# A mixture-of-experts kernel on one core: the order of the routed experts written by hand, and a shared expert in the tail that computes all gates first

## The chip, the cores and the metric

The kernel runs on one core of a Trainium2 chip. The metric is device time in microseconds (us) of one execution. Each number quoted as "the time" is a median of several executions; the profile is one further execution, with the hardware profiler on.

## The reference

Input `x` is four batches of 512 tokens with 512 features, all in float32. There are two residual stages.

```
x = x + tanh(g_xattn) * quantised_mlp(layernorm(x), fside, ctx)      # int8 "smooth quant" GLU, 512 -> 2*256 -> 512
x = x + tanh(g_ffn)   * moe(layernorm(x), gate_w, w_gate, w_up, w_down, ws_gate, ws_up, ws_down)
```

The second stage is a mixture of experts over all 2048 tokens:

```
scores = softmax(x @ gate_w.T)                 # 16 experts; each token takes its best 2
buf[e] = up to 256 tokens that chose expert e  # 16 x 256 x 512
y_e    = (silu(buf[e] @ w_gate[e]) * (buf[e] @ w_up[e])) @ w_down[e]   # 512 -> 352 -> 512
y      = sum over the token's two experts of weight * y_e
sh     = (silu(x @ ws_gate) * (x @ ws_up)) @ ws_down                   # shared expert, 512 -> 704 -> 512
return y + sh
```

## The kernel before, in words

The program is one straight line of instructions, some 6,000 in all, with no loop on the chip. It has five parts.

**Opening (0 to 75 us).** Batch 0 goes through the quantised stage. The order is written out with times (`Program`, lines 43 to 56).

**Plan (75 to 312 us).** Batches 1 to 3 go through the quantised stage, tokens are scored and routed, and the shared expert of batches 0 to 2 fills TensorE between. Each step has an engine, an assumed duration, the steps it needs and a rank. `Plan.run` (lines 83 to 116) keeps a clock for each engine, always takes the step that can begin first, and of those ready on one engine the one with the lowest rank; then it emits the steps in that order. `takes` says that a step needs a free buffer of a kind, `gives` which step frees it; `margin` is how late a TensorE step is assumed to see a result of another engine. Scores and routing have ranks from `ROUTE` = 1e5, the shared expert from `SHARED` = 1e6 (line 1049).

**Routed experts (312 to 551 us).** Loop over 16 experts, lines 1402 to 1419. An expert's gate and up products are done by a Winograd-like scheme: the 512x352 weights are cut in halves, four sums of weight halves (`combine_weights`, four VectorE subtractions, lines 1293 to 1296) and four sums of token halves (`combine_tokens`, lines 1333 to 1336) are formed, and seven products of two matmuls each (`product`, line 1342) replace eight. I number these P1 to P7 in the order of `gate_up`: P1 = b1 from `A11,Bg`, P2 = b2 from `A12,Dg`, P3 adds `S2,T2` onto b1, P4 = b3 from `S1,T1`, P5 adds `S3,T3` onto b1, P6 adds `A22,T4` onto b1, P7 adds `S4,Du` onto b3. Since P3, P5 and P6 accumulate onto b1, ScalarE must have copied b1 out before each of them: `p1` (line 1362) before P3, `u2` (line 1369) before P5, `u3` (line 1372) before P6. Between the copies `p1` and `u2`, ScalarE has the activation `g1` (line 1367), which needs VectorE's sum `p1 + b2` (line 1366).

Between P5 and P6, TensorE transposes the next expert's 256 gathered tokens (`turn_tokens`, `tp_g`, line 1322). After P7 come the down projection of the expert before (`down_routed`, `eo`, line 902) and the transposes of this expert's features (`turn_features`, `tp_h`, line 1391, copied out on VectorE at line 1392 into `ehT`). GpSimd gathers the tokens of expert e+2 by an indirect DMA (`gather`, line 1306). Weights `wg`, `wu`, `wd` of expert e+2 are loaded on the SP queue into one of two buffers each (lines 975 to 980).

Outside a `tc.manual_schedule()` block the framework's own scheduler decides the order of the instructions on each engine, and may put them far from where they stand in the program; inside such a block the order is that of the program. The opening, the plan and the tail are in such blocks; the loop over the experts is not. `combine_weights(e + 1)` stands after P2 of expert e in the program (line 1365), and `routing_weights` (lines 865 to 876: one Exp on ScalarE and nine small VectorE operations, the two combine weights of each token) after expert 1 (line 1419).

**Tail (551 to 625 us).** The shared expert of batch 3, and the gathers of the experts' results. It is 4 chunks of 128 features after chunk 0: for each chunk four gate matmuls (`pg`), Silu, four up matmuls (`pu`), then their product on VectorE into `hT` (line 894); then a rest of 64 features (`pr`, line 926, product at line 933); then four token tiles of six matmuls each (`sh`, line 947), the fifth-numbered chunk being the rest. GpSimd gathers 32 result tiles `yk` (line 1438) into 25 buffers; VectorE adds each to `X` (line 1449), in the order of the token tiles 0 to 15, and each finished tile is stored. How many adds stand ahead of each next step on VectorE is written by hand in line 1459: 6, 13, 19, 21, 26, 28, 30, 32, 32.

Of the kernel before, what the change touches and what calls it, by code (L numbers as in the profile page):

```python
# [20 lines left out]
P = 128  # L21
B, S, H = 4, 512, 512
HC = H // P
# [96 lines left out]
def flamingo_gated_kernel(  # L120
# [758 lines left out]
    def glu_steps(xT, o, dst):  # L879


        v = SimpleNamespace(ps={})
# [6 lines left out]
        def silu():  # L889
            v.g = shp.tile([P, S], F32, tag="g", name="g", bufs=2)  # L890
            act.activation(v.g, v.ps["pg"], AF.Silu)  # L891
# [14 lines left out]
    def shared(b, done=None):  # L906
        s = SimpleNamespace()

        def chunk_steps(c):
            if c == 0:  # L910
                s.hT = shp.tile([P, len(CHUNKS_IS), S], F32, tag="hT", name="hT")
            return glu_steps(xTs[b], c * P, s.hT[:, c, :])
# [30 lines left out]
        def tokens_product(t, c):  # L943
            if c == 0:
# [3 lines left out]
                accs[t], lhsT=s.hT[:m, c, bass.ts(t, P)], rhs=wsd[:m, c, :], start=(c == 0), stop=(c == FULL)  # L948
# [20 lines left out]

    E_W = {}  # L970

    def load_expert(e):
# [4 lines left out]
        nc.sync.dma_start(out=wu, in_=w_up[e].rearrange("(k p) i -> p k i", p=P))  # L977
        wd = ep.tile([P, len(CHUNKS_I), H], F32, tag="wd", name="wd")
        nc.sync.dma_start(out=wd[:, :2, :], in_=w_down[e, : 2 * P, :].rearrange("(c p) h -> p c h", p=P))
        nc.sync.dma_start(out=wd[: I - 2 * P, 2, :], in_=w_down[e, 2 * P :, :])  # L980
        E_W[e] = wg, wu, wd
# [283 lines left out]
    def experts_weights():  # L1265
# [3 lines left out]
        load_expert(0)  # L1269
        load_expert(1)  # L1270

    ep = None
    plan.add("SP", 3.0, experts_weights, firsts[B - 1].last, rank=0.0)
    with tc.manual_schedule():
        planned = plan.run()

    R = [SimpleNamespace() for _ in range(E)]
    HALF = HC // 2

    pair = []

    def combine_weights(e):


        r = R[e]
        wg, wu, _ = E_W[e]  # L1290
        pl, tag = (ep, "T") if e % 2 == 0 else (shp, "hT")
        T = pl.tile([P, 3, HALF, I], F32, tag=tag, name="T", bufs=1)
        vec.tensor_tensor(T[:, 0], wu[:, :HALF, :], wg[:, :HALF, :], ALU.subtract)  # L1293
        vec.tensor_tensor(T[:, 1], wu[:, HALF:, :], T[:, 0], ALU.subtract)
        vec.tensor_tensor(wu[:, :HALF, :], wu[:, HALF:, :], wu[:, :HALF, :], ALU.subtract)
        vec.tensor_tensor(T[:, 2], wg[:, HALF:, :], T[:, 1], ALU.subtract)
        r.T1, r.T2, r.T4, r.T3 = T[:, 0], T[:, 1], T[:, 2], wu[:, :HALF, :]
        r.Bg, r.Dg, r.Du = wg[:, :HALF, :], wg[:, HALF:, :], wu[:, HALF:, :]

    def gather(e):  # L1300
        r = R[e]
        r.xg = []
# [203 lines left out]
```

## Time and profile before

| what | value |
|---|---|
| time before, median of 3 | 621.93 us (621.26 to 623.81) |
| the profiled execution's own time | 627.15 us |
| its span, first to last instruction | 625.4 us |
| TensorE (PE) busy in the span | 572.3 us, 92% |
| VectorE (DVE) busy | 417.1 us, 67% |
| ScalarE (ACT) busy | 169.5 us, 27% |
| GpSimd (POOL) busy | 140.7 us, 22% |
| mean TensorE clock granted | 0.971 of full |
| bytes moved | 83.4 MB, mean 133 GB/s |

How to read it. A float32 matmul appears in the trace as two MATMUL instructions, so four matmuls of a gate chunk are "x8". A line of the timeline gives the start, the time covered, engine, source line, operation, tiles, shapes and count, and in brackets the idle time just before it with what ended that idle time. In the chain of waits a line is start, length and what the end of the program hung on then. In a table of windows the columns are the stretch, its length, TensorE's busy time with its instruction count, the granted clock (1.00 is full), the busy share of the DMA engines, and GB/s. "PEld" is a weight load, which lies beside matmuls. A matmul's end is modelled, so the distance from start to start is the safer measure of what TensorE takes.

### The profile page before, as it was taken

To read this page: it belongs to the slowest core of one execution; us is meant where nothing else is said; L and a number is where in the kernel's file an instruction comes from. 1 tells how busy PE (TensorE), PEld (TensorE's weight loads), DVE (VectorE), ACT (ScalarE), POOL (GpSimd) and SP (SyncE) were. 2 spreads that over 40 slices of the span, in tenths; PEclk is the share of its full clock that TensorE was granted. 3 is DMA by queue.
4 is the path that set the end of the run, shared out by engine and by line. 5 is a ranking of instruction groups with operands and counts; after the bars stand their busy time and mean duration, and the time that the engine had idled before them with its cause. 6 is when DMAs were issued, how large, how long until landed. Compare 5 with 4: busy or idle time off the path is not lost.

```text
span 625.4 us, 6259 instructions
## 1 busy us (share of the span) xinstructions
PE 572.3 (92%) x2068; PEld 309.8 (50%) x2068; DVE 417.1 (67%) x913; ACT 169.5 (27%) x323; POOL 140.7 (22%) x183
## 2 busy tenths in 40 slices
PE   1444999999989999999999999999999999999987
PEld 0322554445545644644365556556556666544422
DVE  6998979999998587473187555556656666313563
ACT  3543354336343520420021222222222222211000
POOL 1223122450432223002021111111111100005770
PEclk9976899999999999899999999999999999999989
DMA  8941110110000450102056666766666664215882
GB/s 304 343 169 40 62 38 31 35 68 1 1 1 0 162 184 1 68 1 67 0 168 214 199 206 214 230 206 212 206 206 205 206 205 127 80 44 163 280 282 105
DMA packets 47103, 83.40 MB, mean 133 GB/s; under 512 B 4880, under 2 KB 23312, under 8 KB 47072
## 3 DMA queue, kind: packets, MB, share of 16 engines
q1 hardware_dynamic: 37344, 57.84, 28.3%
q0 software_dynamic: 5120, 16.78, 9.3%
q10 hardware_dynamic: 4608, 8.39, 3.6%
q8 instruction: 16, 0.26, 0.2%
q14 instruction: 15, 0.12, 0.1%
HBM read 66.23 MB, written 16.78 MB: 133 GB/s over the span
## 4 chain that ended last, share of the span: by engine, by line
PE 66%; DVE 19%; DMA 6%; POOL 4%; issue 3%; ACT 2%; SPq 0%; DVEq 0%; ACTq 0%
PE b L1342 18%; PE sh L947 12%; PE eo L902 9%; PE pg L887 8%; PE pu L887 6%; DMA wu<-in_L_ffn_w_up_dram 4%; POOL yk L1438 3%; PE logit L721 2%; PE tp_g L1322 2%; PE tp_q L353 2%; DVE amw L383 1%; PE tp_x L707 1%; PE acc L533 1%; DMA wi<-in_fside_BxS2xS_dram 1%; DVE bn L284 1%
## 5 line engine op out<-in xcount | busy, mean ns | idle before, releaser
L947 PE MATMUL sh<-wsd,hT 128*128 128x512 f32 x192 | 93.4, 619 | 3.0 <-DVE hT L933 3.0
L902 PE MATMUL eo<-wd,ehT 128*128 128x512 f32 (+1 forms) x192 | 85.3, 592 | 0.0
L887 PE MATMUL pg<-xT,wsg 128*128 128x512 f32 x160 | 78.0, 619 | 0.0
L887 PE MATMUL pu<-xT,wsu 128*128 128x512 f32 x160 | 74.7, 596 | 0.0
L1306 POOL DMA_INDIRECT xg<-xn_dram,slot_token x32 | 31.9, 997 | 145.4 <-PE tp_g L1322 107.9
L902 PEld LDWEIGHTS eo<-wd,ehT 128*128 128x128 f32 (+1 forms) x192 | 36.5, 190 | 41.8 <-issue 38.4
L947 PEld LDWEIGHTS sh<-wsd,hT 128*128 128x128 f32 x192 | 33.7, 192 | 47.2 <-issue 42.2
L1342 PE MATMUL b<-wu,S 128*128 128x352 f32 x128 | 43.9, 466 | 2.3 <-ACT u L1369 2.3
L887 PEld LDWEIGHTS pg<-xT,wsg 128*128 128x128 f32 x160 | 30.0, 197 | 29.8 <-issue 28.8
L887 PEld LDWEIGHTS pu<-xT,wsu 128*128 128x128 f32 x160 | 29.5, 191 | 30.4 <-issue 29.7
L1438 POOL DMA_INDIRECT yk<-eo_dram,slot x32 | 33.6, 1051 | 39.1 <-PE pg L887 29.7
L1399 ACT COPY eo_sb<-eo 128x512 f32<-128x512 f32 x32 | 18.7, 585 | 86.1 <-PE eo L902 62.2
L1342 PE MATMUL b<-wg,xgT 128*128 128x352 f32 x128 | 40.8, 460 | 0.4 <-DVE xgT L1323 0.4
L1342 PE MATMUL b<-T,S 128*128 128x352 f32 x128 | 40.5, 459 | 0.0
L1375 DVE TENSOR_TENSOR u<-u,b 128x352 f32<-128x352 f32 x16 | 8.3, 521 | 43.2 <-ACT u L1372 43.2
L1293 DVE TENSOR_TENSOR T<-wu,wg 128x704 f32<-128x704 f32 x16 | 14.3, 891 | 33.1 <-DMA wu<-in_L_ffn_w_up_dram 33.1
L1449 DVE SCALAR_TENSOR_TENSOR X<-yk,wk,X 128x512 f32<-128x512 f32 x32 | 23.6, 751 | 15.9 <-DMA yk<-eo_dram,slot 15.7
L1342 PEld LDWEIGHTS b<-wu,S 128*128 128x128 f32 x128 | 23.5, 190 | 18.5 <-ACT u L1369 7.3
L891 ACT ACTIVATE g<-pg 128x512 f32<-128x512 f32 x20 | 11.9, 594 | 71.7 <-PE pg L887 71.7
L1342 PEld LDWEIGHTS b<-T,S 128*128 128x128 f32 x128 | 24.4, 190 | 13.5
L953 DVE SCALAR_TENSOR_TENSOR X<-sh,tg_f,X 128x512 f32<-128x512 f32 x16 | 12.0, 747 | 25.3 <-PE sh L947 25.1
L1359 POOL MEMSET h_e<- 128x32 f32 x32 | 4.0, 124 | 110.1 <-PE tp_h L1391 98.8
(207 smaller groups left out, 913.8 us busy)
## 6 DMA issues: line engine op xcount, KB each, us to landing
wg<-in_L_ffn_w_gate_dram SPq DMA_DIRECT2D x16, 704.0 KB, 4.6
wu<-in_L_ffn_w_up_dram SPq DMA_DIRECT2D x16, 704.0 KB, 4.5
wd<-in_L_ffn_w_down_dram SPq DMA_DIRECT2D x16, 512.0 KB, 4.6
eo_dram<-eo_sb ACTq DMA_DIRECT2D x32, 256.0 KB, 3.0
X<-in_x_dram SPq DMA_DIRECT2D x16, 256.0 KB, 8.5
wi<-in_fside_BxS2xS_dram SPq DMA_DIRECT2D x4, 1024.0 KB, 7.3
xn_dram<-y SPq DMA_DIRECT2D x16, 256.0 KB, 2.1
out_dram<-X SPq DMA_DIRECT2D x16, 256.0 KB, 3.9
```

The costliest lines, as they stand in the source:

```text
L353: pe.transpose(tps[k // 2][:, k % 2, t, :], qbits[:, t, bass.ts(k, P)], ident_h)
L721: pe.matmul(pl_t[:, :E], lhsT=xTs[b][:, k, bass.ts(t, P)], rhs=gateT[:, k, :], start=(k == 0), stop=(k == HC - 1),)
L887: pe.matmul(v.ps[name], lhsT=w[:, k, o : o + P], rhs=xT[:, k, :], start=(k == 0), stop=(k == HC - 1))
L902: pe.matmul(acc, lhsT=hT[:m, c, bass.ts(t, P)], rhs=wd[:m, c, :], start=(c == 0), stop=(c == len(chunks) - 1))
L947: pe.matmul(accs[t], lhsT=s.hT[:m, c, bass.ts(t, P)], rhs=wsd[:m, c, :], start=(c == 0), stop=(c == FULL))
L1293: vec.tensor_tensor(T[:, 0], wu[:, :HALF, :], wg[:, :HALF, :], ALU.subtract)
L1306: pool.indirect_dma_start(out=xg, out_offset=None, in_=xn_dram, in_offset=bass.IndirectOffsetOnAxis(ap=slot_token[:, c : c + 1], axis=0),)
L1322: pe.transpose(tp[:, k, :], r.xg[h][:, bass.ts(k, P)], ident)
L1342: pe.matmul(ps[:, :I], lhsT=lhs[:, k, :], rhs=rhs[:, k, :], start=(first and k == 0), stop=(k == HALF - 1), skip_group_check=not first,)
L1399: act.copy(eo, acc)
L1438: pool.indirect_dma_start(out=yk, out_offset=None, in_=eo_dram, in_offset=bass.IndirectOffsetOnAxis(ap=slot[i % 2][:, i // 2 : i // 2 + 1] ...
L1449: vec.scalar_tensor_tensor(X[:, j, :], yks[i], wk[k][:, j : j + 1], X[:, j, :], ALU.mult, ALU.add)
```

## The change

The mathematics is the same. What changes is order and buffers.

1. `load_expert` is split into `load_gate_up` and `load_down`. `load_gate_up(e + 2)` is issued at the end of `gate_up(e)`, `load_down(e + 2)` at the end of `down_routed(e)`. At the start the order is `wg, wu` of experts 0 and 1, then `wd` of both.
2. The loop over the experts stands inside `tc.manual_schedule()`, so its order on every engine is that of the program. `combine_tokens(e + 1)` and `combine_weights(e + 1)` come at the end of `gate_up(e)`, behind P7 and its three VectorE operations. The copies of `turn_features(e)` become a step of their own, `take_features`, that stands in `gate_up(e + 1)` behind `p1 + b2`. The copies of `turn_tokens` become `take_tokens`. `gather(e + 2)` is at the end of `gate_up(e)`.
3. `routing_weights` stays behind expert 1 in the program, but now inside the manual block.
4. Gathers of experts 0 and 1, `combine_weights(0)`, the transposes of expert 0's tokens with their copies, and `combine_tokens(0)` become steps of the plan.
5. In the tail all gates of chunks 1 to 4 come first, then the rest's product, then all ups, with the `g` of these chunks in four new buffers. The gathered results begin with the token tiles of batch 3 (12 to 15) and have 20 buffers, not 25; each add is followed by the next gather. The numbers of adds ahead of the steps are 7, 9, 12, 15, 22, 23, 27, 32. The token tiles 0 and 1 leave chunk 4 to the last: five matmuls each without it, then chunk 4 of both.

The diff, cut to its core:

```diff
-    def glu_steps(xT, o, dst):
+    def glu_steps(xT, o, dst, home):
+        pl, bufs = home
...
-            v.g = shp.tile([P, S], F32, tag="g", name="g", bufs=2)
+            v.g = pl.tile([P, S], F32, tag="g", name="g", bufs=bufs)
...
+    def load_gate_up(e):
...
+    def load_down(e):
...
     def gate_up(e):
...
         product(b1, r.A11, r.Bg, True)
         act.copy(p1, b1[:, :I])
         product(b2, r.A12, r.Dg, True)
-        if e + 1 < E:
-            combine_weights(e + 1)
         vec.tensor_tensor(p1, p1, b2[:, :I], ALU.add)
-        act.activation(g1, p1, AF.Silu)
         product(b1, r.S2, r.T2, False)
+        act.activation(g1, p1, AF.Silu)
         act.copy(u2, b1[:, :I])
+        if e > 0:
+            take_features(e - 1)
         product(b3, r.S1, r.T1, True)
         product(b1, r.S3, r.T3, False)
         act.copy(u3, b1[:, :I])
-        if e + 1 < E:
-            turn_tokens(e + 1)
         vec.tensor_tensor(u3, u3, b3[:, :I], ALU.add)
+        if e + 1 < E:
+            for h in range(CAP // P):
+                turn_tokens(e + 1, h)
+                take_tokens(e + 1, h)
         product(b1, r.A22, r.T4, False)
...
         vec.tensor_tensor(r.h[0][:, :I], g1, u2, ALU.mult)
+        if e + 2 < E:
+            gather(e + 2)
+            load_gate_up(e + 2)
         if e + 1 < E:
             combine_tokens(e + 1)
+            combine_weights(e + 1)
...
-    plan.add("SP", 3.0, experts_weights, firsts[B - 1].last, rank=0.0)
+    weights_there = plan.add("SP", 3.0, experts_weights, firsts[B - 1].last)
+    weights_there = plan.add("DMA", 25.0, nothing, weights_there)
+    plan.margin = 0.6
+    gathered = {}
+    for e in range(2):
+        gathered[e] = plan.add("POOL", 2.6, lambda e=e: gather(e), *ROUTED)
+    there = plan.add("DMA", 4.0, nothing, gathered[0])
+    sums = plan.add("DVE", 3.7, lambda: combine_weights(0), weights_there, rank=ROUTE)
+    home = plan.add("PE", 0.0, open_tokens, there, takes="xT")
+    for h in range(CAP // P):
+        tp = plan.add("PE", 0.55, lambda h=h: turn_tokens(0, h), there, home, takes="tp")
+        turned = plan.add("DVE", 0.7, lambda h=h: take_tokens(0, h), tp, gives=[tp])
+    plan.add("DVE", 1.8, lambda: combine_tokens(0), turned)
     with tc.manual_schedule():
-        planned = plan.run()
-    gather(0)
-    with tc.issue_after(placed[0].ins):
-        combine_weights(0)
-    gather(1)
-    turn_tokens(0)
-    combine_tokens(0)
-    for e in range(E):
-        gate_up(e)
-        if e + 2 < E:
-            gather(e + 2)
-        if e > 0:
-            down_routed(e - 1)
-        if e + 2 < E:
-            load_expert(e + 2)
-        if e < E - 1:
-            turn_features(e)
-        if e == 1:
-            routing_weights(qb)
+        plan.run()
+        for e in range(E):
+            gate_up(e)
+            if e > 0:
+                down_routed(e - 1)
+            if e + 1 < E:
+                turn_features(e)
+            if e == 1:
+                routing_weights(qb)
...
+    tiles = list(range(NT - TT, NT)) + list(range(NT - TT))
     with tc.manual_schedule():
         turn_features(E - 1)
-        last[0]()
+        take_features(E - 1)
+        chunks = [sh3.chunk_steps(0)]
...
         down_routed(E - 1)
-        results = ctx.enter_context(tc.tile_pool(name="results", bufs=25))
+        homes = 20
+        results = ctx.enter_context(tc.tile_pool(name="results", bufs=homes))
...
-        for step, upto in zip(last[1:], (6, 13, 19, 21, 26, 28, 30, 32, 32)):
-            step()
-            for i in range(len(yks), min(2 * NT, upto + 25)):
-                add_results(i - 24)
-                gather_result(i)
+        for c in range(1, FULL):
+            chunks.append(sh3.chunk_steps(c, (results, 4)))
+            for step in chunks[c][0] + [chunks[c][1]]:
+                step()
+        for k in range(HC):
+            sh3.rest_product(k)
+        sh3.rest_silu()
+        for c, upto in zip(range(1, FULL), (7, 9, 12, 15)):
+            for step in chunks[c][2]:
+                step()
             add_results(upto)
+            chunks[c][3]()
+            if c == 2:
+                sh3.rest_times()
+        early = [c for c in range(FULL + 1) if c != FULL - 1] + [FULL - 1]
+        for t, c in [(t, c) for t in range(2) for c in early[:-1]] + [(t, c) for t in range(2) for c in early[-1:]]:
+            sh3.tokens_product(t, c, early)
+        add_results(22)
+        sh3.tokens_add(0)
+        add_results(23)
+        sh3.tokens_add(1)
+        for t, upto in ((2, 27), (3, 2 * NT)):
+            for c in early:
+                sh3.tokens_product(t, c, early)
+            add_results(upto)
+            sh3.tokens_add(t)
```

## The prediction

> **What bounds the kernel now.** I read the table of windows first, then TensorE's timeline over the routed experts and the tail, then the other engines at each of its gaps. TensorE is busy in 92% of the span and from 75 us on it is nearly never without work, so only its gaps and its slow clock can be won; the change removes no matmul. In the chain of waits, the routed loop has pieces like these:
>
> ```profile
> 394.86 4.98 DMA wu<-in_L_ffn_w_up_dram
> 399.93 0.90 DVE T L1293
> 400.86 0.89 DVE T L1294
> 401.75 0.93 DVE ehT L1392 x2
> 403.40 0.89 DVE T L1296
> 405.64 1.45 PE b L1342 x4
> ```
>
> The load of expert e+1's `wu` starts when P7 of expert e-1 has freed its buffer, VectorE starts `combine_weights` the moment it lands, and `p1 + b2`, on which ScalarE's `g1` and then its `u2` copy wait, is queued behind. P5 waits for `u2`. TensorE's timeline shows the same place, and the period:
>
> ```profile
> 385.50 2.53 PE L1342 MATMUL b<-wg,xgT 128*128 128x352 f32 x8
> 400.48 2.53 PE L1342 MATMUL b<-wg,xgT 128*128 128x352 f32 x8
> 402.85 2.53 PE L1342 MATMUL b<-T,S 128*128 128x352 f32 x8
> 405.64 1.45 PE L1342 MATMUL b<-wu,S 128*128 128x352 f32 x4 [0.26 <-ACT u L1369]
> 406.93 1.04 PE L1322 MATMUL tp_g<-ident,xg 128*128 128x128 f32 x8
> 415.98 2.53 PE L1342 MATMUL b<-wg,xgT 128*128 128x352 f32 x8
> ```
>
> Expert 5 takes 14.98 (385.50 to 400.48), expert 6 takes 15.50. 14.97 is the time without a stall: seven products at 1.185, `tp_g` 0.87, `eo` 5.16, `tp_h` 0.65. Expert 2 starts at 338.89 and expert 15 at 537.29: 198.40, less 13 x 14.97 = 194.6, is 3.8 us of stalls.
>
> In the tail VectorE holds TensorE up:
>
> ```profile
> 600.30 0.75 DVE L1449 SCALAR_TENSOR_TENSOR X<-yk,wk,X 128x512 f32<-128x512 f32 x1 [2.03 <-DMA yk<-eo_dram,slot]
> 601.08 0.69 DVE L933 TENSOR_TENSOR hT<-g_rest,pr 64x512 f32<-64x512 f32 x1
> 601.83 19.44 PE L947 MATMUL sh<-wsd,hT 64*128 64x512 f32 x38 [3.04 <-DVE hT L933]
> ```
>
> The rest's product (line 933) stands behind 21 adds, and the last waited 2.03 us for its gather. The table of windows (TensorE alone) shows what follows:
>
> ```profile
> 598.00:602.00 4.00, 0.96 (x3) 1.00 0.91 312
> 602.00:606.00 4.00, 4.00 (x6) 0.63 0.86 259
> 606.00:610.00 4.00, 4.00 (x9) 0.94 0.86 278
> ```
>
> TensorE came back at 0.63 of its clock: 4 x 0.37 + 4 x 0.06 = 1.7 us more. A second slow stretch (0.71, 0.50, 0.93 in the three windows of 4 us from 260) lies at the scores of batch 3: 1.2 + 2.0 + 0.3 = 3.4 us.
>
> **What the Trainium skill says.** "TensorE: Matmul & The Clock Gate", Part 1, has the clock halve after an idle window of about 3.4 us, in windows that run free. The trace agrees: the 3.04 us gap is followed by 0.63, and the gaps of up to 0.91 us in the loop leave 1.00. "TensorE: Matmul & The Clock Gate", Architectural detail, says that ScalarE and VectorE are strictly first in, first out; that is what the chain above shows, `u2` behind `g1` behind `p1 + b2` behind the weights' sums. "ScalarE: Activation LUTs", What ACT_TABLE_LOAD costs, gives about 1283 ns for a load and 1380 ns of drain at each switch of set. The trace has the load and no drain around it:
>
> ```profile
> 265.99 1.28 ACT L868 ACT_TABLE_LOAD   x1 [0.59 <-DVE logits L761]
> 267.28 0.42 ACT L868 ACTIVATE ex<-logits 128x256 f32<-128x256 f32 x1
> 267.72 1.28 ACT L891 ACT_TABLE_LOAD   x1
> 269.01 0.60 ACT L891 ACTIVATE g<-pg 128x512 f32<-128x512 f32 x1
> ```
>
> The second load began while the matmuls its Silu waits for (268.57 by their starts) still ran, so a load need not wait for the operand.
>
> **Part by part.** *Loads (edit 1).* In the trace SP already issues `wg` after P2, `wu` after P7, `wd` after `eo`: the order of the new program. Zero. *Gathers and memsets on GpSimd:* `gather(e + 2)` stands behind two memsets that wait for `tp_h(e - 1)`; it is needed more than 15 us later. Zero.
>
> *Steady loop.* Let t be the end of P7. VectorE: `u2` sum and `h0` to t+1.3 (by 364.92, 0.52 each), four token sums at a pitch of 0.34 to t+2.6, four weight sums of 0.89 to t+6.2. They no longer wait for a load, which now has a full period. The next expert's P1 starts at t+5.81, P2 ends at t+8.2, so `p1 + b2` starts at t+8.4 with 2.2 us to spare. `g1` ends at t+9.4, `u2` at t+10.0, P5 is due at t+10.55: 0.5 us to spare. `ehT` is copied by t+10, the two transpose banks are wanted at t+11.7. P6 wants `u3`: 0.65 after P5, under `tp_g`'s 0.87. No stall is left: -3.8 us. If one of these covers fails, it fails for 13 experts.
>
> *Entry.* Now, TensorE goes from the shared expert's last matmul to `tp_g(0)` and waits 0.64 (312.92 to 313.56) for its copy. In the plan this lies among the 22 us of `sh` matmuls: -0.64. Its gather ends some 6 us after routing (283.4), and the free `xT` buffer comes with the rest's matmuls at 290, so it lands in time. `combine_weights(0)` (3.6 us of VectorE) may go ahead of batch 3's chain once its load is assumed there; the chain then ends at about 287, still 25 us before expert 0. Zero.
>
> *Experts 0 and 1 (now 313.56 to 338.89, 25.33; without stalls 24.74; lost 0.59).* There is no down projection behind expert 0, and the scheduler had put six matmuls of expert 1 there. By hand `tp_h(0)` follows P7 and waits for `h0`: 1.4. Then P3 of expert 1 wants T2 (t+4.6 against t+4.4): 0.2; `p1 + b2` is behind all four sums (t+6.2), `g1` to t+7.2, `u2` to t+7.6, P5 due at 7.0: 0.7. Sum 2.3, so +1.7.
>
> *Routing weights.* The scheduler had put them at 266 to 279, where nothing waited. By hand they stand behind expert 1, on ScalarE behind both `eo` copies, which end with their DMA issue at t+6.3. Table load 1.28 and Exp 0.42: t+8.0. ScalarE's `p1` copy is behind it. VectorE then has 0.42 + 0.25 + 0.23 + 2 x (0.42 + 0.42 + 0.17), with gaps 3.1, to t+11.1; `p1 + b2` to 11.6, `g1` to 12.15, `u2` to 12.6, and P5 was due at 10.55: +2.1. Bounds: if the Silu table is loaded after the wait, 3.4; if the operations pack closer, 1.7. I take 2.1, since the trace shows a load that runs ahead. It is no gain in any case: the old place cost TensorE nothing.
>
> *Expert 15.* There are no next tokens between P5 and P6; the scheduler had put two `eo` matmuls there. By hand P6 waits for the `u3` copy: +0.65.
>
> *Tail.* The same matmuls from 563.42: four `pg` at 3.43, the rest 3.43, four `pu` to 594.32, then 24 `sh` matmuls. In the plan these took 22.06 (289.99 to 312.05, at full clock), so the end is at 616.4; it is at 621.27 now. VectorE's side with the old landings: adds 0 to 6 by 581, product of chunk 1 at 584.8, of chunk 2 at 588.3, the rest's at 588.9, of chunk 4 at 595.2 (wanted at 603). Buffers: gather 20 needs add 0 (572), gather 31 needs add 11 (591), while GpSimd reaches them at 594 and 609: 20 are enough. The last gather lands by 613.5 (12.6 MB at the 290 GB/s of the windows is 43 us from 567, a little more because stores begin later); the five last adds end by 615, before the last tile's matmuls. -4.8 (3.04 of gap and 1.7 of clock).
>
> **Sum**: -3.8 - 0.64 + 1.7 + 2.1 + 0.65 - 4.8 = -4.8 us. On the profiled execution (627.15, span 625.4) that is 622.4. That one was 5.2 above the median of the timed runs, which I take as its own; the difference carries over: 621.93 - 4.8 = **617.2 us**.
>
> **Rivals.** *A, the hand order gives back more:* the Silu table waits (+1.3), and the stall at expert 2 grows to 3.4 and costs clock as in the tail (+1.7): -1.8, 620.1. For it: 3.04 us did just that. Against: the early table load. *B, the clock dip at the scores of batch 3 goes:* the plan from there on is new, and a window with more large matmuls keeps the clock: -4.8 - 3.4, 613.8. For it: the score matmuls of batches 1 and 2 show no dip. Against: the transposes and scores of batch 3 follow each other as closely in the new plan. *C, slower:* in every expert VectorE's queue from P7 to `p1 + b2` comes to lie on the path, since the weights' sums now stand ahead of it. It decides above 9.0 us for that queue, against my 6.2: P5 is late by what is over that. At 9.7 us, 0.7 x 13 = 9.1, and 621.93 - 4.8 + 9.1 = 626.2. Against: no VectorE row for these forms is longer than 0.9 in the loop. *D, no effect:* the scheduler's order is already that of the program where it counts; only the tail changes, and a gather in contention with stores takes two thirds of that back: 620.3. Against: the stalls name a wait that the new order doesn't have.
>
> **Chances.** Forecast 0.50 (616.0 to 618.8), A 0.16, B 0.16, C 0.08, D 0.10. The range runs from B to A and D and a little beyond: 613.4 to 621.2. A measurement of this kernel can tell about 0.5%, 3.1 us, from no change. Faster by more than that (below 618.8): the forecast and B, 0.66. Within: A and D, 0.26. Slower: C, 0.08.
>
> **What would show it.** The period is 14.97 from expert 3 on, with no idle time by `u` in front of P5; VectorE's line 1293 waits for no load. One gap each of about 1.4 ahead of the first `tp_h`, of 2 ahead of expert 2's P5, of 0.65 ahead of expert 15's P6. In the tail no gap ahead of line 947 and a clock of 1.00 to the end. Wrong it would be with a gap in every expert, with an `sh` matmul that waits for `hT`, or with a last tile that waits for a gather.

## The result and the profile after

| | median | of |
|---|---|---|
| before | 623.25 us (621.26 to 630.45) | 22 runs |
| after | 621.22 us (618.44 to 622.48) | 22 runs |
| ratio after to before | 0.9953, 95% interval 0.9934 to 0.9972 | |
| profiled execution of after | 618.44 us, span 616.6, clock 0.98 | 1 |

The gain is 0.47% (0.28 to 0.66%), 2.9 us: small and real, and smaller than the forecast of 4.8. (The ratio weighs every run; the two medians differ by 2.0 us.) The time is 4.0 us above the predicted 617.2. A later comparison gave 621.49 (10 runs) for after and 0.992 (0.9892 to 0.9948), which is 5.0 us. After's own time hardly moved between the two; before's median was 623.25 in the first and 626.57 in the second.

The profiled execution of after shows the routed loop from expert 3 on as the prediction had it. First the chain of waits (start, length, what the end hung on) over expert 6; no load of `wu` and no step of VectorE stands in it:

```profile
397.71 5.92 PE b L1058 x20
403.63 0.87 PE tp_g L1036 x8
404.50 2.37 PE b L1058 x8
406.87 5.16 PE eo L903 x12
412.03 0.66 PE tp_h L1113 x6
```

TensorE's timeline of the same expert has no bracket, that is no idle time, in front of P5 (402.29), and the period is 412.52 - 397.55 = 14.97:

```profile
397.55 2.53 PE L1058 MATMUL b<-wg,xgT 128*128 128x352 f32 x8
399.92 2.53 PE L1058 MATMUL b<-T,S 128*128 128x352 f32 x8
402.29 1.35 PE L1058 MATMUL b<-wu,S 128*128 128x352 f32 x4
403.47 1.04 PE L1036 MATMUL tp_g<-ident,xg 128*128 128x128 f32 x8
...
412.52 2.53 PE L1058 MATMUL b<-wg,xgT 128*128 128x352 f32 x8
```

The shares of the chain of waits went from 66% TensorE (PE), 19% VectorE (DVE) and 6% DMA to these:

```profile
PE 82%; DVE 13%; ACT 2%; issue 1%; DMA 1%; SPq 0%; POOL 0%; ACTq 0%; DVEq 0%
```

What the hand order (edit 2) gives back is in four gaps of TensorE: ahead of the first `tp_h`, in experts 1 and 2 ahead of P5, and in expert 15 ahead of P6.

```profile
319.37 0.85 PE L1113 MATMUL tp_h<-ident,h_e 128*128 128x128 f32 x6 [1.26 <-DVE h_e L1099]
...
325.37 1.45 PE L1058 MATMUL b<-wu,S 128*128 128x352 f32 x4 [0.20 <-ACT u L1083]
...
342.29 1.45 PE L1058 MATMUL b<-wu,S 128*128 128x352 f32 x4 [1.32 <-ACT u L1083]
...
538.93 1.45 PE L1058 MATMUL b<-T,xgT 128*128 128x352 f32 x4 [0.54 <-ACT u L1088]
```

The gap at 342.29 is that of the routing weights. ScalarE's timeline shows that the Silu table was loaded (338.29) ahead of its operand, which came 1.82 after the load's end:

```profile
336.23 1.28 ACT L868 ACT_TABLE_LOAD   x1 [0.39 <-ACT eo_sb L1127]
337.52 0.42 ACT L868 ACTIVATE ex<-logits 128x256 f32<-128x256 f32 x1
337.84 0.43 ACT L1078 COPY p<-b 128x352 f32<-128x352 f32 x1
338.29 1.28 ACT L1082 ACT_TABLE_LOAD   x1
341.40 0.50 ACT L1082 ACTIVATE g<-p 128x352 f32<-128x352 f32 x1 [1.82 <-DVE p L1080]
```

In the tail all 48 `sh` instructions follow each other, and the windows (TensorE alone) have the full clock:

```profile
590.14 22.33 PE L948 MATMUL sh<-wsd,hT 128*128 128x512 f32 x48
```

```profile
598.00:602.00 4.00, 4.00 (x9) 1.00 0.98 343
602.00:606.00 4.00, 4.00 (x10) 1.00 0.93 310
606.00:610.00 4.00, 4.00 (x10) 1.00 0.93 327
```

The spans of the profiled pair differ by 625.4 - 616.6 = 8.8 us. By stages, in us:

| stage | before | after | difference |
|---|---|---|---|
| opening and plan, up to expert 0's first product | 313.56 | 308.68 | -4.88 |
| experts 0 and 1 | 25.33 | 27.03 | +1.70 |
| experts 2 to 14 | 198.40 | 196.60 | -1.80 |
| expert 15 | 14.10 | 14.91 | +0.81 |
| tail, from its first gate product to its last down product | 69.71 | 65.08 | -4.63 |
| the rest | 4.30 | 4.30 | 0.00 |

(The tail is counted to where a next matmul would have begun, 0.17 before the modelled end of the last one.) Of the 4.88, 0.84 were there by 62 us, 3.4 are the slow clock at the scores of batch 3, and 0.65 are the entry. What experts 2 to 14 take above 13 x 14.97 us was 3.75 before and is 1.95 now, all of it in expert 2. So the pair agrees with the working step by step, and the time is nevertheless 4.0 us above the forecast. That is what the runs below are about.

### The profile page after: what moved, and what is told of

Read it like the earlier page. It is cut to its first block, busy times and chain, and to the rows that moved or that the text cites. A ratio compares the mean times of both kernels' runs of the same rounds, so it can differ in the third digit from the quotient of the medians.

```text
span 616.6 us, 6231 instructions
## 1 busy us (share of the span) xinstructions
PE 566.7 (92%) x2068; PEld 307.6 (50%) x2068; DVE 421.7 (68%) x913; ACT 170.4 (28%) x323; POOL 139.8 (23%) x183
## 4 chain that ended last, share of the span: by engine, by line
PE 82%; DVE 13%; ACT 2%; issue 1%; DMA 1%; SPq 0%; POOL 0%; ACTq 0%; DVEq 0%
PE b L1058 20%; PE eo L903 13%; PE sh L948 13%; PE pg L888 10%; PE pu L888 10%; PE tp_g L1036 2%; PE pr L927 2%; PE logit L721 2%; PE tp_q L353 2%; PE acc L533 2%; PE tp_h L1113 1%; PE tp_x L707 1%; DMA wi<-in_fside_BxS2xS_dram 1%; DVE xn L465 1%; PE rowb L299 1%
## 5 line engine op out<-in xcount | busy, mean ns | idle before, releaser
L948 PE MATMUL sh<-wsd,hT 128*128 128x512 f32 (+1 forms) x192 | 92.0, 610 | 0.0
L888 PE MATMUL pg<-xT,wsg 128*128 128x512 f32 x160 | 74.1, 600 | 0.0
L948 PEld LDWEIGHTS sh<-wsd,hT 128*128 128x128 f32 (+1 forms) x192 | 32.9, 189 | 42.7 <-issue 42.1
L1486 DVE SCALAR_TENSOR_TENSOR X<-yk,wk,X 128x512 f32<-128x512 f32 x32 | 23.2, 749 | 17.4 <-DMA yk<-eo_dram,slot 17.2
L1080 DVE TENSOR_TENSOR p<-p,b 128x352 f32<-128x352 f32 x16 | 8.3, 520 | 32.7 <-PE b L1058 32.7
L1058 PEld LDWEIGHTS b<-wg,xgT 128*128 128x128 f32 x128 | 23.1, 190 | 10.9 <-issue 0.8
```

The costliest lines, as they stand in the source:

```text
L888: pe.matmul(v.ps[name], lhsT=w[:, k, o : o + P], rhs=xT[:, k, :], start=(k == 0), stop=(k == HC - 1))
L948: pe.matmul(accs[t], lhsT=s.hT[:m, c, bass.ts(t, P)], rhs=wsd[:m, c, :], start=(c == order[0]), stop=(c == order[-1]),)
L1058: pe.matmul(ps[:, :I], lhsT=lhs[:, k, :], rhs=rhs[:, k, :], start=(first and k == 0), stop=(k == HALF - 1), skip_group_check=not first,)
L1486: vec.scalar_tensor_tensor(X[:, j, :], yks[added[0]], wk[k][:, j : j + 1], X[:, j, :], ALU.mult, ALU.add)
```

## The experiments

In the expectations, T is the theory at the time that the terms seen in the profiled pair hold in most executions; R1 is the rival that the old tail loses less in most executions than in the profiled one; R2 that the hand order costs more in most. All ratios are to the kernel before, timed in the same comparison; these runs belong to three comparisons, each on a chip of its own, in which before's median was 624.98 (61 runs), 626.57 (23) and 627.18 (25) in turn. "Stall" is what experts 2 to 14 take above 13 x 14.97 us; the tail is counted as above. These stages are read in one profiled execution of each run.

| run | median, us (runs) | ratio (95% interval) | experts 0 and 1 | stall | expert 15 | tail |
|---|---|---|---|---|---|---|
| before, first profile | | | 25.33 | 3.75 | 14.10 | 69.71 |
| before, second profile | 621.97 (1) | | 25.31 | 2.57 | 14.10 | 67.09 |
| new tail alone | 622.51 (22) | 0.996 (0.994 to 0.998) | 26.38 | 4.72 | 14.10 | 65.08 |
| old tail in after | 622.98 (22) | 0.9966 (0.9947 to 0.9986) | 27.03 | 1.96 | 14.91 | 66.73 |
| weights in the plan | 619.85 (8) | 0.9909 (0.9875 to 0.9944) | 27.04 | 0.00 | 14.91 | 65.08 |
| before, other numbers | 625.57 (22) | 1.001 (0.9987 to 1.0032) | 26.09 | 5.47 | 14.10 | 64.89 |
| before, stores last | 632.6 (9) | 1.0093 (1.006 to 1.0126) | 26.87 | 5.13 | 14.09 | 66.05 |
| after again | 621.49 (10) | 0.992 (0.9892 to 0.9948) | 27.04 | 1.95 | 14.91 | 65.09 |
| sums behind P2 | 631.78 (11) | 1.0087 (1.0055 to 1.0118) | 31.39 | 7.84 | 14.91 | 65.09 |
| experts 0 and 15 mended | 616.06 (6) | 0.9842 (0.9802 to 0.9881) | 24.89 | 0.01 | 14.10 | 65.08 |
| the same, gathers early | 616.57 (4) | 0.9837 (0.9777 to 0.9896) | 24.89 | 0.01 | 14.09 | 65.09 |

**The new tail alone** is the kernel before with edit 5 (of the tail's loop the core):

```diff
-        for step, upto in zip(last[1:], (6, 13, 19, 21, 26, 28, 30, 32, 32)):
+        for c, upto in zip(range(1, FULL), (7, 9, 12, 15)):
+            for step in chunks[c][2]:
+                step()
+            add_results(upto)
```

> The kernel before, with only the tail of the changed kernel (gates first, batch 3's tiles first, 20 buffers). Theory T (the parts add as worked out, and the median moved less because single executions differ in where the clock dips): no gap ahead of a token-tile matmul, clock 1.00 to the end, 4.8 us faster than before, ratio 0.992. Rival R1 (the tail of a usual execution of the kernel before loses less than the profiled one did): 2 to 3 us faster, ratio 0.9955, and the kernel before shows a smaller gap in its tail. Rival R2 (the tail is worth 4.8, but the loop ordered by hand costs some 2 us more in a usual execution than in the profiled one): 4.8 us faster, and the next run is slower than before.

Measured: 0.996 (0.994 to 0.998) of 624.98, so 2.5 us (1.2 to 3.7), not the 4.6 of the profiled pair. The tail is at 65.08, as in after.

**The old tail in after** takes edit 5 back and leaves edits 1 to 4:

```diff
-        for c, upto in zip(range(1, FULL), (7, 9, 12, 15)):
+        for step, upto in zip(last[1:], (6, 13, 19, 21, 26, 28, 30, 32, 32)):
```

> The changed kernel with the tail of the kernel before. T and R1: entry -0.64, loop +0.65, so within 0.5 us of before, ratio 1.000. R2: 2 us slower than before, ratio 1.003, with a stretch of reduced clock behind the 2 us gap of expert 2.

Measured: 0.9966, so edits 1 to 4 gain about 2.1 us (0.9 to 3.3) by themselves. That speaks against R2, and it is more than T and R1 had for them, 0.5 us at most. The two halves add up to 4.6 us in this comparison. In the profile the old tail lost 66.73 - 65.08 = 1.65 us. Its timeline on VectorE and TensorE shows why:

```profile
596.85 0.75 DVE L1480 SCALAR_TENSOR_TENSOR X<-yk,wk,X 128x512 f32<-128x512 f32 x1 [1.96 <-DMA yk<-eo_dram,slot]
...
598.25 1.12 PE L948 MATMUL sh<-wsd,hT 128*128 128x512 f32 x2 [0.59 <-DVE hT L895]
...
599.56 0.69 DVE L934 TENSOR_TENSOR hT<-g_rest,pr 64x512 f32<-64x512 f32 x1
...
600.30 17.75 PE L948 MATMUL sh<-wsd,hT 64*128 64x512 f32 x38 [0.92 <-DVE hT L934]
```

It is the same wait, an add for its gather with the hT products behind, but in two gaps of 0.59 and 0.92, and 38 `sh` matmuls take 17.75 in place of 19.44: the clock stayed up. The profiled before had 3.04 in one gap and paid for it twice.

**Before again** is that kernel once more, for a second profile.

> The kernel before once more, for one more profiled execution. Theory: experts 2 to 15 stall by 3.7 to 5.5 us again, in experts whose up weights took over 4.8 us to land; the tail from its first gate product to its last down product loses between 1.0 and 4.7 us against 65.08, so that what the changed tail is worth is a draw of the execution. Rival (the profile of before was the usual one): a gap of 3.0 us in the tail and stalls of 3.75 us, within 0.3.

Measured: a span of 620.2, against 625.4. Its tail:

```profile
596.29 1.12 PE L947 MATMUL sh<-wsd,hT 128*128 128x512 f32 x2 [0.95 <-DVE hT L894]
598.33 17.75 PE L947 MATMUL sh<-wsd,hT 64*128 64x512 f32 x38 [0.92 <-DVE hT L933]
```

Two gaps of 0.95 and 0.92, full clock, a loss of 2.01. So the old tail's loss is a draw, which differs from execution to execution: 4.63 was one, 1.65 and 2.01 are two others, as R1 has it. This execution, at 621.97 us, was however among the fastest of before: the median of 25 runs of its comparison is 627.18, which is the time of the first profile (627.15). What the old tail loses in most executions is thus better read from the new tail alone, 2.5 us. The stall of 2.57 lies below the range expected, 3.7 to 5.5.

**After again:**

> The changed kernel once more, beside the other kernels of this call. T: in the segments of the trace nothing but the clock at the scores of batches 1 and 3 and the opening moves: 27.03 from expert 0 to 2, 196.6 from 2 to 15, 14.9 to the tail, 65.1 in the tail. R1 says the same of this kernel and places the spread in the kernel before. R2: at least one slow stretch behind the gap at expert 2.

The routed stage and the tail repeat to 0.01 us. Expert 0 begins at 312.98 where the first profile had 308.68. Of these 4.3 us, 2.3 are there by 75 us, from the opening that both kernels share, and 2.0 arise between 137 and 184 us, where the clock dips:

```profile
136.00:140.00 4.00, 3.05 (x10) 0.74 0.53 197
140.00:144.00 4.00, 4.00 (x21) 0.84 0.17 66
```

Fifteen of the 18 profiles, of either order, have one such dip: at 136 to 144 us, where it costs 1.8 to 2.0 us from matmul to matmul (12 profiles), or at 260 to 272, where it costs 1.7 (two profiles) or 3.4. The 3.4 is that of the first profile of before. The first profile of after had no dip.

**Other numbers in the old tail** (6, 13, 16, 16, 19, 26, 29, 32, 32). It leaves out that batch 3's tiles are stored with all their results: the last are added after the store.

```diff
-        for step, upto in zip(last[1:], (6, 13, 19, 21, 26, 28, 30, 32, 32)):
+        for step, upto in zip(last[1:], (6, 13, 16, 16, 19, 26, 29, 32, 32)):
```

> The kernel before with five other numbers of adds ahead of the tail's steps: 6, 13, 16, 16, 19, 26, 29, 32, 32 in place of 6, 13, 19, 21, 26, 28, 30, 32, 32, so that the products of chunk 4 and of the rest stand behind 16 adds, not 19 and 21. T: the 3.04 us gap and the 1.7 us of reduced clock behind it go without gates first and without the new order of tiles, 4.5 us faster, ratio 0.993. Rival: adds that stand behind a token tile's add then become late and the end waits for a gather, 1 to 2 us faster only, 0.997.

Measured: 1.001, no difference. TensorE's gap in the tail is gone (64.89), but from its last matmul to the end it is 7.77 us, not 4.30, since VectorE has the late adds still to do, and they wait for the stores of their tiles:

```profile
615.11 2.20 DVE L1449 SCALAR_TENSOR_TENSOR X<-yk,wk,X 128x512 f32<-128x512 f32 x3 [4.77 <-DMA out_dram<-X]
...
620.32 2.20 DVE L1449 SCALAR_TENSOR_TENSOR X<-yk,wk,X 128x512 f32<-128x512 f32 x3 [2.16 <-DMA out_dram<-X]
```

With these numbers alone the wait only moves to the end. Numbers that keep every add ahead of its store were not run.

**Stores last** in the old tail, to take them from beside the gathers:

```diff
-                if k == 1 and j < NT - TT:
-                    store(j)
...
             add_results(upto)
+        for j in range(NT - TT):
+            store(j)
```

> The kernel before with the stores of token tiles 0 to 11 issued behind the last step of the tail and not between the adds. T and R1 (the gap in the old tail is the landing of gathers 17 to 20 in contention with stores, so its size differs between executions): no gap ahead of a token-tile matmul, the tail's matmuls end 65.1 us after its first, as in the changed kernel; 12 stores of 256 KB at 290 GB/s then end some 11 us behind the last add, so the whole is 4 to 7 us slower than before. Rival (gathers are late by GpSimd's own pace): the gap stays at 1.5 to 3.

Measured: a gap of 1.08 is left where 0.9 to 3.04 was, so the stores are not what makes the gathers late, or only a part of it. GpSimd issues the gathers without a pause in both runs, one each 1.25 to 1.7 us (575 to 600 us), so its own pace, the rival, is part of it at least. The end lies 13.09 us behind the last matmul, 8.8 more than before, which is more than the whole loss.

**Weights in the plan**: the Exp and the nine VectorE operations become two steps of the plan.

```diff
+    ex = plan.add("ACT", 3.0, weights_exp, *ROUTED, rank=ROUTE)
+    plan.add("DVE", 3.1, weights_sums, ex, rank=ROUTE + 400)
...
-            if e == 1:
-                routing_weights(qb)
```

> The changed kernel with the routing weights (one Exp, nine small VectorE operations) as steps of the plan behind the routing of batch 3, not behind expert 1. T: the gap ahead of expert 2's fifth product (1.32 shown, 1.95 over the period) goes, 2.0 us faster than the changed kernel; against before 0.9953 less 0.0032, 0.992. R2: more than that, 3.5 to 4 us, 0.9895. A rival that the gap is hidden by something else: 0.9953.

Measured: expert 2 is at 14.97 (16.92 before this edit), the stall is 0.00. The 1.95 is gone, and nothing came in its place. (The interval of the ratio holds T's 0.992 and R2's 0.9895 alike; it is the period that decides.)

**Experts 0 and 15 mended**, on top of that:

```diff
         product(b2, r.A12, r.Dg, True)
+        if e == 1:
+            turn_features(0)
         vec.tensor_tensor(p1, p1, b2[:, :I], ALU.add)
+        if e == 0:
+            combine_weights(1)
...
+        else:
+            begin_down(e - 1)
         product(b1, r.A22, r.T4, False)
...
-            if e + 1 < E:
+            if 0 < e < E - 1:
                 turn_features(e)
```

`begin_down(14)` issues the first `eo` matmul of expert 14 between P5 and P6 of expert 15.

> On top of the routing weights in the plan: the weights' sums of expert 1 stand behind expert 0's p1 + b2, the feature transposes of expert 0 behind expert 1's second product, and the first matmul of expert 14's down projection between the fifth and the sixth product of expert 15. T: the gaps of 1.26 and 0.9 at experts 0 and 1 and of 0.65 at expert 15 go, no idle time of TensorE is left between expert 0 and the end of the tail; 2.9 us faster than with the routing weights alone, against before 0.986 to 0.987. Rival: VectorE becomes late at expert 1 all the same, 1 us faster only.

Measured: 24.89 and 14.10, so 27.04 - 24.89 + 0.81 = 2.96 us less, as expected; 616.06 and a ratio of 0.9842. From expert 0 on TensorE has no gap left. This version and the next are the best of the study.

**Sums behind P2** puts the weights' sums back to where before has them, ahead of `p1 + b2`, under the hand order:

```diff
         product(b2, r.A12, r.Dg, True)
+        if e + 1 < E:
+            combine_weights(e + 1)
         vec.tensor_tensor(p1, p1, b2[:, :I], ALU.add)
...
-            combine_weights(e + 1)
```

> The changed kernel with the sums of the next expert's weights back at their place in the kernel before, behind the second product, ahead of p1 + b2. T: VectorE waits for the load of wu again and the stretch from expert 2 to expert 15 gets the 3.75 to 5.5 us of stalls of the kernel before, plus nothing at experts 0 and 1 or up to 1 us less there; 3 to 4 us slower than the changed kernel, 1.000 to 1.002 of before. Rival (the loop's gain came from the manual order as a whole, not from the place of these sums): as the changed kernel, 0.995.

Measured: slower by 0.87%, and not as the prediction's reason has it. Experts 0 to 2 lose all of it: 31.39 - 27.04 = 4.35 us in experts 0 and 1, and 7.84 - 1.95 = 5.89 in expert 2. In expert 1 P5 waits 2.45. In expert 2 the sums are queued behind the routing weights, P5 waits 4.66, and the clock is at 0.50 and 0.69 in the two windows from 352. Experts 3 to 14 have no stall at all, although VectorE waits for `wu` in each:

```profile
455.21 0.89 DVE L1007 TENSOR_TENSOR T<-wu,wg 128x704 f32<-128x704 f32 x1 [2.29 <-DMA wu<-in_L_ffn_w_up_dram]
...
458.62 0.52 DVE L1082 TENSOR_TENSOR p<-p,b 128x352 f32<-128x352 f32 x1
459.06 1.01 DVE L1121 COPY ehT<-tp_h 128x384 f32<-128x384 f32 x2
...
460.72 1.35 PE L1058 MATMUL b<-wu,S 128*128 128x352 f32 x4
```

So the place of the sums alone is not what stalled the old loop.

**Gathers early**, on the mended version. The old order issued the gathers of expert e+3 as soon as `tp_g` of expert e+1 was done, 2.6 and 1.3 us ahead of the load of `wu`; the hand order issues them at the start of the next expert.

```diff
+            if e == 1:
+                gather(3)
+            if e > 0 and e + 3 < E:
+                gather(e + 3)
...
-            gather(e + 2)
+            if e < 1:
+                gather(e + 2)
```

> The version of the experts 0 and 15 run, with the gathers of expert e+3 issued right behind the turning of expert e+1 (from expert 1 on), as the order of the kernel before had them, and the sums still at the end of the expert. Theory G (the old loop's stalls come from gathers that run beside the load of the up weights, when the sums behind P2 wait for that load): the load takes 5.0 to 5.7 us to land in place of 4.3, the sums at the end don't notice, TensorE keeps 14.97 us per expert, and the time is that of the experts 0 and 15 run, 616.1, within 1 us. Rival S (the place of the gathers means nothing, landing stays 4.3): same time, landing 4.3. The two part on the landing alone.

Measured: `wu` lands 4.2 to 5.9 us after its issue (median 4.5) where it took 4.2 to 4.5 (median 4.3) without the gathers ahead of it; no expert is longer, since the sums stand at the end and begin 17.4 us after the issue. The spread is the gathers' doing. The other profiles agree: over the loads for experts 3 to 15, 31 of 91 took more than 4.8 us in the seven profiles with early gathers, and 1 of 91 in seven with late ones.

**Two misses.** To cross the place of the sums with that of the gathers, I put the sums behind P2 from expert 2 on, once with early and once with late gathers:

```diff
         vec.tensor_tensor(p1, p1, b2[:, :I], ALU.add)
-        if e == 0:
-            combine_weights(1)
+        if e + 1 < E and e != 1:
+            combine_weights(e + 1)
```

> Both together: gathers right behind the turning of tokens, and from expert 2 on the sums of the next expert behind P2. Theory G: the sums wait for the slowed load for more than the cover that they have, so the steady stalls of the kernel before come back by themselves: some experts of 15.4 to 15.9 us, 3 to 5.5 us in all over experts 2 to 15, and about 620 us. Rival S (the stalls came from the rest of the order that was the scheduler's, such as the place of the feature copies or of u3's add): all experts at 14.97 and 616 us.

> From expert 2 on the sums of the next expert stand behind P2, the gathers stay at the start of the following expert. Theory G: VectorE waits for the up weights in every expert, up to 2.3 us, the load lands 4.3 us after its issue, no expert is over 15.0 us, and the time is 616 us. The prediction's own reason (the sums behind P2 are what stalls the loop): stalls of 3 to 5.5 us over experts 2 to 15 and about 620 us.

Measured: 632.35 and 632.29, both 1.0083 (1.0059 to 1.0106 and 1.0053 to 1.0114), and 16.17 us in every expert of both from expert 2 to 14. The edit was one line too low: the sums stood behind `p1 + b2`, not ahead of it. That costs 1.20 per expert by another way, whatever the gathers do. In the run with late gathers:

```profile
340.02 0.89 DVE L1011 TENSOR_TENSOR T<-wu,wg 128x704 f32<-128x704 f32 x1
...
343.35 1.02 DVE L1131 COPY ehT<-tp_h 128x384 f32<-128x384 f32 x2
...
344.01 1.09 PE L1040 MATMUL tp_g<-ident,xg 128*128 128x128 f32 x8 [0.98 <-PE b L1062]
```

The feature copies end late behind the sums, and `tp_g` wants the PSUM buffers that they free. The wait is put down to PE, which had long been done at that time; the copy at 343.35 is what came just before. The runs tell nothing of the old stalls.

**The four that cross it rightly**: sums ahead of `p1 + b2` from expert 2 on in all four, gathers early or late, and the feature copies of the expert before behind `p1 + b2` (hand order) or between the sums and `p1 + b2`. In the chain quoted in the prediction such a copy stands among the sums (401.75, line 1392). All four leave expert 2's own sums at the end of expert 1. The edit that puts the copies ahead, beside that of the sums:

```diff
+        if 1 < e < E - 1:
+            combine_weights(e + 1)
+            take_features(e - 1)
         vec.tensor_tensor(p1, p1, b2[:, :I], ALU.add)
...
-        if e > 0:
+        if e in (1, E - 1):
             take_features(e - 1)
```

> On the version of the experts 0 and 15 run: from expert 2 on the sums of the next expert stand ahead of p1+b2, where the kernel before has them, and the gathers go out right behind the turning of tokens. The feature copies stay behind p1+b2, as the hand order has them. Theory C (a stall is the landing of the up weights less what VectorE has to spare before p1+b2 is late: 4.47 us with the two feature copies ahead of p1+b2, read from the stalls of the kernel before, and 4.47 + 0.93 = 5.4 without): landings of 4.2 to 5.9 us, a stall only where one is above 5.4, 0 to 1.5 us over experts 2 to 15, about 617. Theory G alone (the gathers are all of it): 3 to 5.5 us, about 620.

> The same place of the sums, ahead of p1+b2 from expert 2 on, with the gathers at the start of the following expert and the feature copies behind p1+b2. Theories C and G: landings of 4.2 to 4.4 us, no stall, 616. The prediction's reason (sums in that place are what stalls the loop): 3 to 5.5 us of stalls, about 620.

> All three as the kernel before has them, from expert 2 on: sums ahead of p1+b2, gathers right behind the turning, and the feature copies of the expert before between the sums and p1+b2. Theory C: the stalls of the kernel before come back, each its landing less 4.47 us: 3 to 6 us over experts 2 to 15 and 619 to 622. Rival: still something else of the scheduler's order is needed, and experts stay at 14.97.

> Sums and feature copies ahead of p1+b2, gathers late. Theory C: landings of 4.2 to 4.4 us stay just under 4.47, so no stall but for a landing that strays, 0 to 0.8 us in all, about 616.5. If the copies ahead of p1+b2 are the whole cause, whatever the gathers do: 3 us and more, 619 to 622.

| gathers | feature copies | expert 2 above 14.97 | experts 3 to 14 above | median (4 runs) |
|---|---|---|---|---|
| early | behind `p1 + b2` | 0.32 | 0.00 | 622.89 us |
| late | behind `p1 + b2` | 0.33 | 0.01 | 622.15 us |
| early | ahead | 1.25 | 3.56 | 628.12 us |
| late | ahead | 1.26 | 0.01 | 622.03 us |

(These four are from a comparison of their own, on another chip. Their tails, whose code is that of after, took 67.9 to 69.0: in each, VectorE sat idle for 9 to 10 us ahead of its last `hT` product, which no other run shows; what for, the trace doesn't say. So only the routed stage is compared, and the medians among the four.) Only with all three as the old order had them do the stalls of experts 3 to 14 come back, 3.56 us, or 4.81 with expert 2, as theory C expected. Here is expert 11 with copies ahead and gathers early. VectorE begins the sums 5.57 us after the load's issue at 469.50, P5 waits, and the expert takes 16.0 us:

```profile
475.07 0.89 DVE L1011 TENSOR_TENSOR T<-wu,wg 128x704 f32<-128x704 f32 x1 [3.01 <-DMA wu<-in_L_ffn_w_up_dram]
...
478.41 1.02 DVE L1139 COPY ehT<-tp_h 128x384 f32<-128x384 f32 x2
479.34 0.51 DVE L1089 TENSOR_TENSOR p<-p,b 128x352 f32<-128x352 f32 x1
480.77 1.45 PE L1062 MATMUL b<-wu,S 128*128 128x352 f32 x4 [0.75 <-ACT u L1094]
```

And here is expert 3 of the run with the copies behind and gathers early. Its load was nearly as late, the sums begin 5.42 us after the issue at 346.70, and P5 has no bracket; the expert takes 14.97:

```profile
352.12 0.89 DVE L1011 TENSOR_TENSOR T<-wu,wg 128x704 f32<-128x704 f32 x1 [2.86 <-DMA wu<-in_L_ffn_w_up_dram]
...
355.46 0.51 DVE L1088 TENSOR_TENSOR p<-p,b 128x352 f32<-128x352 f32 x1
355.89 1.02 DVE L1138 COPY ehT<-tp_h 128x384 f32<-128x384 f32 x2
357.06 1.35 PE L1062 MATMUL b<-wu,S 128*128 128x352 f32 x4
```

This one expert carries the case for the copies in the steady loop: with the copies ahead its load would have cost some 0.9 us (by the rule that follows), the other loads of that run 0.2 at most.

The sizes close. In the two profiles of before, an expert's stall is the landing of its `wu` less 4.47 us: landings of 5.0, 5.3, 5.6 and 5.9 went with 0.53, 0.87, 1.19 and 1.41, and up to 4.5 with 0.00 to 0.09. The two copies take 0.93 (401.75 in the prediction's chain), and in expert 2 moving them behind takes 1.25 - 0.32 = 0.93 off. Expert 2's own excess fits too. There VectorE comes to the sums 5.8 us after the issue with no idle time before, straight from expert 2's own sums. The sums of the steady loop begin 0.1 after a landing, so this is as late as a landing of 5.7 us, and 5.7 - 4.47 is 1.23 with the copies ahead and, less 0.93, 0.30 with them behind: 1.25 and 0.32 were measured. One part is not measured: that the early gathers delay the load by sharing the DMA engines is argued from their place and the landings.

## Why the prediction was wrong, point by point

**Loads, gathers and memsets: zero.** Right under the new order: with the gathers early the mended version has 0.9837, without 0.9842. In the old order the place of the gathers did count, as the next point shows.

**Steady loop: -3.8.** Size right in the pair (3.75, and 0.00 left beside the routing weights); over five profiles with the old order it was 2.57, 3.75, 4.72, 5.13 and 5.47, so 4.3 in the mean. The cover that the prediction gave `p1 + b2`, 2.2 us, is 2.38 in the trace. The reason was too narrow. The prediction has it that the sums no longer wait for a load, and this does hold: with early gathers and the sums at the end no expert stalled (tested with the copies behind `p1 + b2` only). But with the sums left where they were, late gathers alone remove the stalls of experts 3 to 14, and so do the copies behind `p1 + b2` alone. The prediction took the gathers as a step with no effect and did not read the copy that stood among the sums in its own lines.

**Entry: -0.64.** Right: the gap ahead of expert 0 is gone. **Experts 0 and 1: +1.7.** Right in the pair (+1.70). The old order itself took 25.31 to 26.87 there, so against the mean of five, 26.0, it is +1.0. **Routing weights: +2.1.** Measured 1.95, and the early table load held. **Expert 15: +0.65.** Measured 0.81.

**Tail: -4.8.** Here is the term that was mis-sized: the new tail alone measured -2.5 (1.2 to 3.7). It took 65.08 or 65.09 in nine profiles (and 67.9 to 69.0 in the four on the other chip), and the mechanism was right: without the wait the clock stays up. But what it replaces differs from execution to execution. The prediction took the 3.04 gap and the 1.7 of clock behind it as what the old tail costs; the same code lost 1.65 and 2.01 in two other profiles.

**The sum and its base.** The failing step is the sentence "That one was 5.2 above the median of the timed runs, which I take as its own; the difference carries over". It sets the 5.2 aside as that execution's own, and carries the stalls of that same execution over in full, to a base of three faster runs. Both halves failed.

The base first. 621.93 was the median of three runs. The same kernel had 623.25 (22 runs), and 624.98, 626.57 and 627.18 in the later comparisons, while after stayed at 621.22 and 621.49. So the base was 1.3 to 5.3 us too low, and the 627.15 that was put down to one execution is no more than the median of one of these comparisons. Why before differs so much between comparisons stays open; the later ones each ran on a chip of their own.

Then the sum, -4.8. (It is 4.79, so that the time should have read 617.1.) With the means of the profiles for the stages that vary (loop 4.3; experts 0 and 1 1.0; tail 2.8, of 4.63, 2.01 and 1.65) it is -4.3 - 0.65 + 1.0 + 1.95 + 0.8 - 2.8 = -4.0 us. That lies within both measurements, 2.9 us (1.7 to 4.1) and 5.0 (3.3 to 6.8). By parts it was off both ways: edits 1 to 4 come to 0.0 in the prediction (-3.8 - 0.64 + 1.7 + 2.1 + 0.65) and gained 2.1, the tail comes to 4.8 and gained 2.5. That these two nearly cancel, to 4.6, is luck. By the medians of the first comparison, 1.3 of the 4.0 us are the base and 2.7 the sum; by those of the second, 626.57 to 621.49, the sum is right and the whole miss is the base. The runs don't decide between the two.

**Rivals.** *A* did not come: the table was loaded early, and the gap of 1.32 at expert 2 left the clock alone. *B* came in the pair (the dip of 3.4 was gone) and fell with the other profiles: two runs with the new plan dip at the scores of batch 3, and four of five with the old plan don't. The dip belongs to the execution; no run shows that larger matmuls keep the clock. *C* did not come under this order; its kin did when the sums stood behind `p1 + b2`, at 1.20 per expert, by way of the feature copies. *D* fell too: the order of the experts did change the time (0.9966 without the new tail), and stores took nothing of the new tail back. A and D were nearest in size (620.1 and 620.3), for reasons that the runs don't bear out.

**The clock.** The prediction says that the trace agrees with the page that it cites. It does so only in part: the gap of 3.04 us is shorter than the idle window given there, the clock went down behind gaps from 2.14 us on, and at 264 to 268 in the first profile of before it was at 0.50 with no gap ahead of it.

## What to carry to other kernels

If the profiled execution lies above the median of a few runs, find out first which of the two is usual: time more runs, and take a second profile. Its surplus sits in some of the very stalls that are priced, so price each stall by its least and its usual size before a difference is carried to a median. When a queue is reordered, list all that moved in it: here either of two moves was enough by itself for the steady loop, and only the crossed runs told that. A step moved out of a place where nothing waited (the routing weights, the first transposes) costs what its new place can't cover, and mending that gave 5.4 us by the medians of one comparison (621.49 to 616.06), where the whole change had given 5.1.

## What the runs showed of the hardware

- A load of 704 KB landed in 4.1 to 5.2 us (median 4.3, one of 91 above 4.8) in seven profiles with no gather issued just ahead of it, and in 4.1 to 6.6 us (median 4.5, 31 of 91 above 4.8) in seven with two gathers issued 2.6 and 1.3 us ahead.
- TensorE's clock went down behind each gap of 2.14 to 4.66 us in the routed loop and the tail (2.14, 2.19, 2.26, 2.45, 3.04 and 4.66; the lowest 4 us window after them had 0.50 to 0.77), and stayed at 1.00 behind gaps of up to 1.50 there. Near 136 us all 18 profiles have the same gap of 1.34 or 1.35, and the clock went down behind it in 12 of them. It also went to 0.50 for 4 us at 264 to 268 in the first profile of before, while TensorE was busy in the whole window. So the length of the gap alone doesn't decide; what does stays open.
- A switch of ScalarE's table cost the 1.28 us of the load and no more (the Exp began at 337.52, after a load from 336.23), and the load ran ahead of the operand.
